# A graph kernel with listed neighbours: one own and four shared gather slots a block in place of three and two

## The chip, the cores and the metric

The kernel runs on one core of one Trainium2 chip. The metric is device time in microseconds of one execution. Three runs of the kernel before gave 667.77, 664.38 and 665.90 us; the median is 665.9 us. The core's engines are named as in the profile: PE (TensorE, matmul), ACT (ScalarE), DVE (VectorE), POOL (GpSimd) and SP (SyncE, which only issues DMAs here).

## The reference

A graph of 4096 nodes with 512 features and an adjacency matrix of 4096 x 4096 integers, in which an entry is 1 with probability 0.000976562, so that a row has four neighbours on average. Two layers, each followed by a residual and a layer normalization:

```python
# layer 0: graph attention, 8 heads of 64
Wh = jnp.einsum('nf,hfo->hno', x, W)
f1 = jnp.einsum('hno,ho->hn', Wh, a[:, :F_OUT])
f2 = jnp.einsum('hno,ho->hn', Wh, a[:, F_OUT:])
e = jax.nn.leaky_relu(f1[:, :, None] + f2[:, None, :], ALPHA)
e = jnp.where(adj[None, :, :] > 0, e, NEG_INF)
attn = jax.nn.softmax(e, axis=-1)
out = jnp.einsum('hnm,hmo->hno', attn, Wh)
x = layernorm(x + out)                     # heads side by side
# layer 1: neighbour mean
mask = (adj > 0).astype(x.dtype)
deg = jnp.sum(mask, axis=1, keepdims=True)
agg = mask @ x / jnp.maximum(deg, 1.0)
combined = jnp.concatenate([x @ W_self + b_self, agg @ W_nb + b_nb], axis=-1)
x = layernorm(x + relu(combined @ W_comb + b_comb))
```

## The kernel before

The kernel never multiplies by the adjacency matrix. It turns each row of it into a list of at most 16 neighbours and then fetches the neighbours' rows from a table in DRAM. If a list doesn't fit, a flag is set and a dense version (`dense_layers`) runs after it; with these inputs it doesn't.

**Blocks and slots.** The 4096 nodes are 32 blocks of 128, one node per partition. For each block the kernel issues five gathers (`gather`, L628, through `rows_of`, L618): each is an indirect DMA that POOL issues and that fetches one table row into each of the 128 partitions, into one of five slots of a buffer `g`. The first `K0 = 3` slots are a node's own: neighbour 1, 2 and 3 of the node that sits on the partition. The last `KH = 2` slots are shared: all further neighbours of the block's first 64 nodes are packed one after another into the 128 places of the first shared slot, those of the other 64 into the second. For each shared place the kernel keeps who owns it (`es`), and the matrix `own` with a 1 where place p belongs to node c lets PE add the shared rows to their owners.

**Stage 1, the lists** (L930 to L968, and the rest up to L1006). Per block, SP loads 2 MB of adjacency, ACT turns it into a mask with a row sum (`mask_adj`, L424), PE folds it into keys (`fold_adj`, L438) and DVE takes the largest ones (`max_keys`). For every four blocks `decode` (L461) makes the lists: it counts the degrees, computes where each node's further neighbours start (the matmul with `triuh`), builds a placing matrix of 128 x 256 per block (L517, L518), and moves the entries into their shared places with one matmul per block and shared slot (L524). `own` is stored as bytes (L547). Beside that, PE computes the table rows of layer 0 (`node_half`, L371): eight values f2, then 512 features; they are stored in the DRAM table `t0`.

**Stage 2, attention** (the loop at L1023). It is a software pipeline written out by hand: iteration i works on blocks i - 1 to i + 6, and each engine runs its instructions in the order in which they are written. For a block, in the order of the data:
- five gathers into one of `GA = 5` buffers; `gather(i + 6)` is issued after the shared matmuls of block i + 1, whose buffer it takes;
- DVE: `a_weights` (L648) adds f1 and f2 and applies the leaky ReLU;
- ACT: `a_exp` (L653) takes the exponential twice: of all five slots into the PSUM tile `ew`, and of the shared slots into the buffer's first eight columns;
- DVE: `a_weigh` (L665) multiplies two slots by their weights, in place, called once for the shared and once for own slots 2 and 3; `a_first` (L672) multiplies own slot 1 into the PSUM tile `num`; `a_own_sum` (L684) and `a_adds` (L689) add the own weights and rows;
- PE: `a_shared` (L696) adds the shared rows, for each half of the columns and each shared slot one matmul whose output is 64 partitions (`tile_position=(0, k * HP)`);
- DVE: `a_recip`; ACT: `a_scale` (L711) divides the eight heads, one instruction each; DVE: `a_moments`; ACT: `root` and `norm` (L727 to L739);
- PE and ACT: transposes of the normalized block (`transposed`, L347), the product with the neighbour weights (`a_z`, L741), stored in table `t1`.

In this stage PSUM's eight banks are `num` (two tiles of two banks), one `ew`, one `tp`, two `pw`.

**Stage 3, layer 1** (L1077 on; the loop at L1133). Five gathers from `t1` per block into one of `GB = 7` buffers. ACT copies own slot 1 into PSUM (`g_first`, L755), DVE adds own slots 2 and 3 (`g_adds`, L759) and makes the owners' matrix (`owners`, L607), PE adds the shared rows (`g_shared`, L781) to the bias and to the product with the self weights (`g_self`, L774), DVE combines both (`g_moments`, L799) and ACT normalizes (`g_norm`). A gather of block b + 7 is issued after `g_adds` of block b. For the first six blocks, gathers are issued during stage 2 for the rows of `t1` that exist by then (`gather_early`), and the missing rows are added later (`g_late`).

A gather waits for whoever last read the slot that it fills: in stage 3 that is ACT for the first slot, DVE for the second and third, PE for the shared ones.

Of the kernel before, what the change touches and what calls it, by code (L numbers as in the profile page):

```python
# [31 lines left out]
F32 = mybir.dt.float32  # L32
BF16 = mybir.dt.bfloat16
# [3 lines left out]
OP = mybir.AluOpType  # L37
# [3 lines left out]
P = 128  # L41
# [8 lines left out]
K0 = 3  # L50
KH = 2
# [62 lines left out]
def listed_layers(  # L114
# [58 lines left out]
    triuh = const.tile([P, P], BF16, name="triuh")  # L173
    nc.vector.tensor_copy(triuh, triu)
    nc.vector.memset(triuh[0:HP, HP:P], 0.0)
    slot = const.tile([P, KH], F32, name="slot")
    for k in range(KH):
        for c in range(KH):
            nc.vector.memset(slot[k * HP : (k + 1) * HP, c : c + 1], float((k + c) * P))
    iota = const.tile([P, KH * P + 1], F32, name="iota")  # L180
    nc.gpsimd.iota(
        iota, [[1, KH * P + 1]], base=0, channel_multiplier=0,
        allow_small_or_imprecise_dtypes=True,
    )
    pidx = const.tile([P, KH], F32, name="pidx")
    nc.gpsimd.iota(
        pidx, [[P, KH]], base=0, channel_multiplier=1, allow_small_or_imprecise_dtypes=True
# [62 lines left out]
    es = const.tile([P, NB, KH, EX], F32, name="es")  # L250
# [210 lines left out]
    def decode(b0, dp, place):  # L461
# [46 lines left out]
        nc.tensor.matmul(po, lhsT=triuh, rhs=nx, start=True, stop=True)  # L508
        nc.vector.tensor_scalar(L[:, :, KL], po, slot[:, 0:1], None, OP.add)
# [3 lines left out]
        for b in range(b0, b0 + G):  # L513
            io, off, en = iota[:, 0 : KH * P], lst[:, b, KL : KL + 1], end[:, b : b + 1]
            lt = dp.tile([P, KH * P], F32, name="lt", bufs=1)
            st = place(b)
            nc.vector.tensor_scalar(lt, io, en, None, OP.is_lt)  # L517
            nc.vector.scalar_tensor_tensor(st, io, off, lt, OP.is_ge, OP.mult)  # L518
            sts.append(st)
            yield  # L520
        pe = ps.tile([P, G, KH, EX + H], F32, name="sm", bufs=2)
        for g in range(G):
            for k in range(KH):
                nc.tensor.matmul(  # L524
                    pe[:, g, k, :], lhsT=sts[g][:, ts(k, P)], rhs=lst[:, b0 + g, K0:],
                    start=True, stop=True,
                )
        nc.vector.tensor_copy(es[:, bs], pe[:, :, :, 0:EX])
        nc.vector.tensor_copy(f1s[:, bs, K0:KS, :], pe[:, :, :, EX:])
        kx = dp.tile([P, G, KH], F32, name="kx", bufs=1)  # L530
        nc.vector.tensor_tensor(
            kx, pidx.unsqueeze(1).to_broadcast([P, G, KH]), es[:, bs, :, KX], OP.subtract
        )
# [6 lines left out]
        nc.vector.tensor_mul(  # L540
            jk, jk, es[:, bs].rearrange("p g k c -> p (g k) c")[:, :, 0:KX]
        )
# [9 lines left out]
            es[:, bs, :, KX + 2 : KX + 3].to_broadcast([P, G, KH, HP]),  # L552
# [4 lines left out]
    def late_lists(dp, place):  # L557
# [21 lines left out]
        for b in range(NE):  # L579
            lt = dp.tile([P, KH * P], F32, name="lt", bufs=1)  # L580
            nc.vector.tensor_scalar(lt[:, 0:P], iota[:, 0:P], endl[:, b : b + 1], None, OP.is_lt)
            nc.vector.scalar_tensor_tensor(
                place[:, b, :], iota[:, 0:P], tl[:, b, KL : KL + 1], lt[:, 0:P], OP.is_ge, OP.mult
            )
            if b % 2:
                yield
# [20 lines left out]
    def owners(b, pool):  # L607

        s = pool.tile([P, KH, P], F32, name="own", bufs=4)[:, :, 0:HP]
        for k in range(KH):  # L610
            E = es[:, b, k, :]
            nc.vector.tensor_scalar(
                s[:, k, :], iota[:, 1 + k * HP : 1 + (k + 1) * HP], E[:, KX + 2 : KX + 3],
                E[:, KX + 1 : KX + 2], OP.is_equal, OP.mult,
            )
        return s
# [27 lines left out]
    def a_owners(b, wp):  # L644
        OWN[b] = wp.tile([P, KH, P], F32, name="own", bufs=4)[:, :, 0:HP]
        nc.scalar.copy(OWN[b], own[:, b])  # L646
# [6 lines left out]
    def a_exp(b):  # L653

        e = E[b]
        w = E[b] = ps.tile([P, KS, H], F32, name="ew")
        nc.scalar.activation(w, e, AF.Exp)
        nc.scalar.activation(G0[b][:, K0:KS, 0:H], e[:, K0:KS, :], AF.Exp)
# [25 lines left out]
    def a_own_sum(b):  # L684
        nc.vector.tensor_reduce(
            NM[b][:, 0:H], E[b][:, 0:K0, :].rearrange("p k h -> p h k"), AX.X, OP.add
        )

    def a_adds(b):  # L689
        for k in range(1, K0):  # L690
            nc.vector.tensor_add(  # L691
                halves_of(NM[b]), halves_of(NM[b]),
                G0[b][:, k, H:TW].rearrange("p (a c) -> p a c", a=2),
            )
# [16 lines left out]
    def a_scale(b):  # L711

        for h in range(H):
            a, q = divmod(h, H // 2)
            o = a * HD + (1 - a) * H + q * D
            s = NM[b][:, o : o + D]
            nc.scalar.mul(s, s, RD[b][:, h : h + 1])  # L717

# [36 lines left out]
    def g_first(b, g):  # L755
        Y[b] = ps.tile([P, HD], F32, name="sm", bufs=2)
        nc.scalar.copy(Y[b], g[:, 0, 0:HD])

    def g_adds(b, g, wp):  # L759
        yp = Y[b]  # L760
        nc.vector.tensor_add(yp, yp, g[:, 1, 0:HD])
        Y[b] = wp.tile([P, HD], F32, name="y", bufs=2)
        nc.vector.tensor_add(Y[b], yp, g[:, 2, 0:HD])  # L763
# [17 lines left out]
    def g_shared(b, g):  # L781
        for a in range(2):
            for k in range(KH):
                r = slice(a * HH, (a + 1) * HH)
                nc.tensor.matmul(
                    NM[b][ts(k, HP), r], lhsT=OWN[b][:, k, :], rhs=g[:, K0 + k, r],
                    start=False, stop=True, tile_position=(0, k * HP), skip_group_check=True,
                )
# [10 lines left out]
    def g_moments(b):  # L799
        yp = ps.tile([P, HD], F32, name="sm", bufs=2)  # L800
        nc.vector.scalar_tensor_tensor(  # L801
            yp, Y[b], lst[:, b, KL + 1 : KL + 2], NM[b], OP.mult, OP.add
        )
        mu = MV[b] = small.tile([P, 1], F32, name="ln_sum")
        nc.vector.scalar_tensor_tensor(
            Y[b], yp, 0.0, xs[:, b, :], OP.max, OP.add, accum_out=mu
        )
# [111 lines left out]
    def on_own(b):  # L919
        return wp.tile([P, KH * P], F32, name="own", bufs=4)  # L920
# [4 lines left out]
    last = oo.tile([P, G, KH * P], F32, name="last")  # L925
# [81 lines left out]
    ps.stage(dict(num=2, ew=1, tp=1, pw=2), dict(sm="tp", mp="pw"))  # L1007
# [15 lines left out]
    for i in range(-3, NB + 2):  # L1023
# [13 lines left out]
        if on(i + 2):  # L1037
            a_first(i + 2)
            a_weigh(i + 2, slice(1, K0))
            a_own_sum(i + 2)  # L1040
            a_adds(i + 2)
# [7 lines left out]
        if i == 21:  # L1049
            lists = [late_lists(dp, last.rearrange("p g (a k) -> p (g a) k", a=2))]  # L1050
# [46 lines left out]
    for b in range(2):  # L1097
        g_bias(b)
        g_first(b, G1[b])
        g_shared(b, G1[b])  # L1100
        g_adds(b, G1[b], wq)
# [22 lines left out]
    nc.vector.tensor_scalar(bad[:, 2, :], end, slot[:, 1:2], None, OP.is_gt)  # L1124
# [8 lines left out]
    for b in range(NB):  # L1133
        if b > 1:
            g_first(b, G1[b])
# [11 lines left out]
        if b > 1:  # L1147
            g_adds(b, G1[b], wq)
            if b + GB < NB:
                G1[b + GB] = gather(t1, b + GB, gps[b % GB])  # L1150
            if b + 2 < NB:
                OWN[b + 2] = owners(b + 2, wp)
        g_moments(b)
# [403 lines left out]
```

## Time and profile before

| What | us |
|---|---|
| median of three runs | 665.9 |
| profiled execution, its own time | 773.3 |
| its span, first to last instruction | 771.6 |
| stage 1, to about | 215 |
| start of attention | 215 to 284 |
| attention | 284 to 500 |
| layer 1, start | 500 to 571 |
| layer 1, with gathers | 571 to 733 |
| layer 1, last blocks | 733 to 771 |

The profiled execution is 107 us longer than the median. In the lines of the profile a line number is that of the kernel before; `out<-in` are the program's names; `x` counts instructions; after the bar stand the busy time in all, the mean of one in nanoseconds, and the idle time of the engine just before these instructions with what ended most of it. In a listing in order of time the first number is the start, the second the duration, and the bracket at the end holds the idle time before it and its releaser. "issue" is a wait that nothing in the profile explains, "remote" one whose release was not recorded. Issuing a DMA is not counted as busy time, except for POOL's indirect ones, where the busy time is that of generating the descriptors and not of the transfer.

### The profile page before, as it was taken

What the parts mean: (1) busy time and instruction counts of PE and PEld (TensorE: products, weight loads), DVE (VectorE), ACT (ScalarE), POOL (GpSimd) and SP (SyncE); (2) the same over time, 40 slices, a digit from 0 to 9 for tenths busy, and PEclk for the clock granted to TensorE, in tenths of its full rate; (3) what the DMA queues carried; (4) which work ended last, traced back from release to release, by engine and by line L of the source; (5) the groups of instructions that cost most, each with busy time, mean ns of one, the idle gap of its engine ahead of it and who ended that gap; (6) DMA issues with size and microseconds to landing.
All of it is one profiled execution on the core that took longest, in us unless ns stands there. A gap on an engine that the chain in (4) does not pass through costs nothing.

```text
span 771.6 us, 9266 instructions
## 1 busy us (share of the span) xinstructions
PE 592.0 (77%) x2358; PEld 312.3 (40%) x2358; DVE 461.5 (60%) x1267; ACT 490.6 (64%) x1313; POOL 354.4 (46%) x474
## 2 busy tenths in 40 slices
PE   5799889889975277877779867956599678877783
PEld 2466666656632033333334333423243223333231
DVE  6256868677743589876788879503036433444373
ACT  3688888889650377887778879722045444554484
POOL 4111121111247565655666752574526666766600
PEclk9899999999998579988889989888799889888997
DMA  8999999999987478897777874685548777888741
GB/s 274 404 408 408 407 408 408 409 408 400 406 291 209 135 222 257 235 319 247 236 235 227 263 228 162 222 268 180 171 123 273 238 255 256 277 262 260 252 161 59
DMA packets 92038, 209.65 MB, mean 272 GB/s; under 512 B 13694, under 2 KB 13702, under 8 KB 91978
## 3 DMA queue, kind: packets, MB, share of 16 engines
q0 software_dynamic: 28624, 94.39, 40.0%
q1 hardware_dynamic: 63024, 114.05, 39.7%
q10 hardware_dynamic: 330, 0.54, 0.2%
q8 instruction: 21, 0.34, 0.2%
q14 instruction: 39, 0.32, 0.1%
HBM read 175.25 MB, written 33.69 MB: 271 GB/s over the span
## 4 chain that ended last, share of the span: by engine, by line
ACT 23%; PE 21%; DMA 18%; another core or an unknown queue 17%; DVE 10%; issue 9%; SPq 1%; ACTq 0%; DVEq 0%
DMA at<-in_adj_dram 16%; ACT num L717 6%; PE tp L312 4%; ACT ab L426 3%; PE pw L744 3%; PE pw L374 3%; PE pw L776 3%; ACT xs L739 3%; ACT xs L730 2%; PE nm L776 2%; DVE sm L801 2%; ACT xT L359 2%; DVE y L763 2%; ACT ln_rs L733 1%
## 5 line engine op out<-in xcount | busy, mean ns | idle before, releaser
L619 POOL DMA_INDIRECT g<-t,idx x290 | 277.6, 957 | 173.1 <-issue 78.1
L744 PE MATMUL pw<-wr,xT 128*128 128x512 f32 x256 | 141.8, 705 | 42.7 <-ACT xT L359 31.7
L426 ACT ACTIVATE ab<-at 128x2048 bf16<-128x2048 int32 x64 | 122.5, 1915 | 34.2 <-DMA at<-in_adj_dram 32.0
L374 PE MATMUL pw<-w_sb,xT 128*128 128x264 f32 x512 | 130.4, 400 | 6.4 <-issue 3.8
L374 PEld LDWEIGHTS pw<-w_sb,xT 128*128 128x128 f32 x512 | 94.6, 194 | 33.3 <-issue 7.1
L744 PEld LDWEIGHTS pw<-wr,xT 128*128 128x128 f32 x256 | 54.8, 225 | 116.1 <-issue 77.9
L381 POOL COPY lst<-row 128x8 f32<-128x8 f32 x32 | 6.6, 205 | 164.8 <-DVE row L378 164.8
L776 PE MATMUL nm<-m,xT 128*128 128x512 f32 x128 | 66.1, 664 | 18.7 <-DMA xT<-xt 13.6
L717 ACT ACTIVATE num<-num,rd 128x64 f32<-128x64 f32 x256 | 73.1, 286 | 9.5 <-DVE rd L709 2.1
L667 DVE TENSOR_TENSOR g<-g,ew 128x1024 f32<-128x1024 f32 x64 | 77.5, 1212 | 0.2
L776 PE MATMUL pw<-m,xT 128*128 128x512 f32 x128 | 64.6, 651 | 16.5 <-DMA xT<-xt 15.2
L801 DVE SCALAR_TENSOR_TENSOR sm<-y,lst,nm 128x512 f32<-128x512 f32 x16 | 12.1, 753 | 84.8 <-remote 37.7
L701 PE MATMUL num<-g,own 128*64 128x264 f32 (+1 forms) x256 | 37.8, 419 | 27.8 <-ACT own L646 15.8
L378 DVE COPY row<-pw 128x264 f32<-128x264 f32 x64 | 27.3, 427 | 34.4 <-PE pw L374 24.2
L776 PEld LDWEIGHTS nm<-m,xT 128*128 128x128 f32 x128 | 26.1, 213 | 52.9 <-issue 31.7
L691 DVE TENSOR_TENSOR num<-num,g 128x512 f32<-128x512 f32 x64 | 44.8, 699 | 2.2
L776 PEld LDWEIGHTS pw<-m,xT 128*128 128x128 f32 x128 | 25.5, 208 | 50.1 <-issue 32.9
L353 PE MATMUL tp<-ident,xs 128*128 128x128 f32 x256 | 40.6, 283 | 6.6 <-ACT xT L366 2.4
L748 ACT COPY row<-pw 128x512 f32<-128x512 f32 x32 | 18.7, 586 | 41.5 <-remote 25.4
L353 PEld LDWEIGHTS tp<-ident,xs 128*128 128x128 f32 x256 | 31.9, 146 | 30.6 <-issue 16.6
L619 POOL DMA_INDIRECT g<-t,idxe x30 | 28.5, 949 | 27.1 <-DVE rd L709 12.3
L767 ACT COPY nm<-brow 128x512 f32<-128x512 f32 x16 | 9.4, 585 | 45.8 <-issue 23.3
(221 smaller groups left out, 951.2 us busy)
## 6 DMA issues: line engine op xcount, KB each, us to landing
at<-in_adj_dram SPq DMA_DIRECT2D x64, 1024.0 KB
xt<-xT SPq DMA_DIRECT2D x32, 256.0 KB
t<-row SPq DMA_DIRECT2D x32, 256.0 KB
xT<-xt SPq DMA_DIRECT2D x32, 256.0 KB
out_dram<-row SPq DMA_DIRECT2D x32, 256.0 KB
t<-row POOLq DMA_DIRECT2D x31, 260.0 KB
xs<-in_x_dram SPq DMA_DIRECT2D x31, 256.0 KB
g<-t,idx POOLq DMA_INDIRECT x290
```

Of the source, the lines that this page charges most:

```text
L312: nc.tensor.matmul(mp, lhsT=wT[:, d, :], rhs=wc[:, d, :], start=(d == 0), stop=(d == FB - 1))
L353: nc.tensor.transpose(tp[:, c, :], xs[:, b, ts(c, P)], ident)
L374: nc.tensor.matmul(pw, lhsT=xT[:, c, :], rhs=w_sb[:, c, k * HW : (k + 1) * HW], start=(c == 0), stop=(c == FB - 1),)
L426: nc.scalar.activation(ab, loads.pop((b, h)), AF.Relu, accum_out=asum[:, b, h : h + 1])
L619: nc.gpsimd.indirect_dma_start(out=out, out_offset=None, in_=table, in_offset=bass.IndirectOffsetOnAxis(ap=at, axis=0),)
L667: nc.vector.tensor_tensor(gv, gv, E[b][:, sl].unsqueeze(3).to_broadcast([P, sl.stop - sl.start, H, D]), OP.mult,)
L691: nc.vector.tensor_add(halves_of(NM[b]), halves_of(NM[b]), G0[b][:, k, H:TW].rearrange("p (a c) -> p a c", a=2),)
L701: nc.tensor.matmul(NM[b][ts(k, HP), a * HD : a * HD + r.stop - r.start], lhsT=OWN[b][:, k, :], rhs=G0[b][:, K0 + k, r], start=False, stop= ...
L717: nc.scalar.mul(s, s, RD[b][:, h : h + 1])
L744: nc.tensor.matmul(pz, lhsT=xT[:, c, :], rhs=m2[:, c, :], start=(c == 0), stop=(c == FB - 1))
L776: nc.tensor.matmul(NM[b], lhsT=xT[:, c, :], rhs=m1[:, c, :], start=False, stop=(c == FB - 1), skip_group_check=True,)
L801: nc.vector.scalar_tensor_tensor(yp, Y[b], lst[:, b, KL + 1 : KL + 2], NM[b], OP.mult, OP.add)
```

## The change

`K0` becomes 1 and `KH` 4: a node has one own slot, and each quarter of a block (32 nodes) has one shared slot of 128 places. The number of gathers stays five. `KX`, the length of the shared part of a list, grows from 13 to 15.

- `decode`: the placing matrix is 128 x 128 for all four slots together. To keep the slots apart, the lists are first multiplied by `part`, which is 1 for a row's own quarter, into `lq`; one matmul per block then fills all four slots.
- `a_exp`: one exponential, from `e` into the first eight columns of the gathered buffer, which is in SBUF; `ew` is gone, and its PSUM bank becomes a second `tp`. `a_weigh` is called once, for the four shared slots; it and `a_first` read the weights from the buffer.
- `a_adds` and `g_adds` are gone; `a_own_sum` is a copy.
- `a_shared` and `g_shared`: matmuls with an output of 32 partitions at four column positions, eight in attention, four of 512 columns in layer 1 (before: four of 264 or 256).
- `a_scale`: ACT divides four heads, DVE the other four in one instruction.
- Layer 1: `g_moments` reads own slot 1 straight from the gathered buffer, except for blocks 0 and 1, where `g_first` copies it into SBUF; so the gather of block b + 7 is now issued after `g_moments` of block b. `owners` is two instructions over all four slots.

```diff
-K0 = 3
-KH = 2
+K0 = 1
+KH = 4
...
-        po = ps.tile([P, G], F32, name="sm", bufs=2)
-        nc.tensor.matmul(po, lhsT=triuh, rhs=nx, start=True, stop=True)
-        nc.vector.tensor_scalar(L[:, :, KL], po, slot[:, 0:1], None, OP.add)
+        nc.tensor.matmul(po, lhsT=triuq, rhs=nx, start=True, stop=True)
+        nc.vector.tensor_copy(L[:, :, KL], po)
...
-            io, off, en = iota[:, 0 : KH * P], lst[:, b, KL : KL + 1], end[:, b : b + 1]
-            lt = dp.tile([P, KH * P], F32, name="lt", bufs=1)
+            io, off, en = iota[:, 0:P], lst[:, b, KL : KL + 1], end[:, b : b + 1]
+            lt = dp.tile([P, P], F32, name="lt", bufs=1)
...
+        lq = dp.tile([P, G, KH, EX + H], F32, name="lq", bufs=1)
+        nc.vector.tensor_tensor(
+            lq, lst[:, bs, K0:].unsqueeze(2).to_broadcast([P, G, KH, EX + H]),
+            part.unsqueeze(1).unsqueeze(3).to_broadcast([P, G, KH, EX + H]), OP.mult,
+        )
         pe = ps.tile([P, G, KH, EX + H], F32, name="sm", bufs=2)
         for g in range(G):
-            for k in range(KH):
-                nc.tensor.matmul(
-                    pe[:, g, k, :], lhsT=sts[g][:, ts(k, P)], rhs=lst[:, b0 + g, K0:],
-                    start=True, stop=True,
-                )
+            nc.tensor.matmul(
+                pe[:, g].rearrange("p k c -> p (k c)"), lhsT=sts[g],
+                rhs=lq[:, g].rearrange("p k c -> p (k c)"), start=True, stop=True,
+            )
...
     def owners(b, pool):
-        s = pool.tile([P, KH, P], F32, name="own", bufs=4)[:, :, 0:HP]
-        for k in range(KH):
-            E = es[:, b, k, :]
-            nc.vector.tensor_scalar(
-                s[:, k, :], iota[:, 1 + k * HP : 1 + (k + 1) * HP], E[:, KX + 2 : KX + 3],
-                E[:, KX + 1 : KX + 2], OP.is_equal, OP.mult,
-            )
+        s = pool.tile([P, KH, HP], F32, name="own", bufs=4)
+        nc.vector.tensor_tensor(
+            s, iota[:, 1 : P + 1].rearrange("p (k c) -> p k c", k=KH),
+            es[:, b, :, 1:2].to_broadcast([P, KH, HP]), OP.is_equal,
+        )
+        nc.vector.tensor_tensor(s, s, es[:, b, :, 0:1].to_broadcast([P, KH, HP]), OP.mult)
...
     def a_exp(b):
-        e = E[b]
-        w = E[b] = ps.tile([P, KS, H], F32, name="ew")
-        nc.scalar.activation(w, e, AF.Exp)
-        nc.scalar.activation(G0[b][:, K0:KS, 0:H], e[:, K0:KS, :], AF.Exp)
+        e, E[b] = E[b], G0[b][:, :, 0:H]
+        nc.scalar.activation(E[b], e, AF.Exp)
...
     def a_scale(b):
-        for h in range(H):
-            a, q = divmod(h, H // 2)
-            o = a * HD + (1 - a) * H + q * D
-            s = NM[b][:, o : o + D]
+        for h in range(H // 2):
+            s = NM[b][:, H + h * D : H + (h + 1) * D]
             nc.scalar.mul(s, s, RD[b][:, h : h + 1])
+        s = NM[b][:, HD : HD + HH].rearrange("p (h d) -> p h d", d=D)
+        nc.vector.tensor_tensor(
+            s, s, RD[b][:, H // 2 :].unsqueeze(2).to_broadcast([P, H // 2, D]), OP.mult
+        )
...
     def g_shared(b, g):
-        for a in range(2):
-            for k in range(KH):
-                r = slice(a * HH, (a + 1) * HH)
-                nc.tensor.matmul(
-                    NM[b][ts(k, HP), r], lhsT=OWN[b][:, k, :], rhs=g[:, K0 + k, r],
-                    start=False, stop=True, tile_position=(0, k * HP), skip_group_check=True,
-                )
+        for k in range(KH):
+            nc.tensor.matmul(
+                NM[b][ts(k, HP), :], lhsT=OWN[b][:, k, :], rhs=g[:, K0 + k, 0:HD],
+                start=False, stop=True, tile_position=(0, k * HP), skip_group_check=True,
+            )
...
-    ps.stage(dict(num=2, ew=1, tp=1, pw=2), dict(sm="tp", mp="pw"))
+    ps.stage(dict(num=2, tp=2, pw=2), dict(sm="tp", mp="pw"))
...
             a_first(i + 2)
-            a_weigh(i + 2, slice(1, K0))
             a_own_sum(i + 2)
-            a_adds(i + 2)
...
         if b > 1:
-            g_first(b, G1[b])
+            Y[b] = G1[b][:, 0, 0:HD]
             g_shared(b, G1[b])
...
         if b > 1:
-            g_adds(b, G1[b], wq)
-            if b + GB < NB:
-                G1[b + GB] = gather(t1, b + GB, gps[b % GB])
             if b + 2 < NB:
                 OWN[b + 2] = owners(b + 2, wp)
-        g_moments(b)
+        g_moments(b, wq)
+        if b > 1 and b + GB < NB:
+            G1[b + GB] = gather(t1, b + GB, gps[b % GB])
```

## The prediction

> **What bounds the kernel now.** I read the page's busy row and its chain first, then busy time by stretch, then the costliest groups, then single instructions in order of time.
>
> ```profile
> PE 592.0 (77%) x2358; PEld 312.3 (40%) x2358; DVE 461.5 (60%) x1267; ACT 490.6 (64%) x1313; POOL 354.4 (46%) x474
> ...
> ACT 23%; PE 21%; DMA 18%; another core or an unknown queue 17%; DVE 10%; issue 9%; SPq 1%; ACTq 0%; DVEq 0%
> ```
>
> No engine is full and the chain changes hands all the time: the stages have different limits. The 17% (some 131 of 771.6 us) are waits whose end no record shows. The profiled execution took 773.3 us and the median is 665.9 us, 107 us less; most of those waits probably belong to the profiling. So I count differences per block in stretches without such a wait, and carry them over one to one.
>
> ```profile
> 284.00:500.00 216.00, 171.72 (x598) 79.97 (x599) 174.10 (x384) 173.07 (x566) 125.03 (x131) 0.88 0.76 238
> 500.00:571.00 71.00, 47.49 (x120) 21.68 (x120) 10.80 (x34) 18.31 (x44) 35.88 (x38) 0.83 0.60 183
> 571.00:733.00 162.00, 128.42 (x394) 52.48 (x392) 73.85 (x164) 81.66 (x208) 107.94 (x114) 0.88 0.81 258
> 733.00:771.00 38.00, 24.31 (x90) 10.19 (x88) 22.53 (x48) 25.21 (x66) 1.21 (x2) 0.89 0.33 111
> ```
>
> Columns: length, then busy PE, PE load, DVE, ACT, POOL, then clock, DMA share, GB/s. The first stretch is layer 0's attention, the last two are layer 1. In attention three engines stand at 0.8. The 215 us ahead of it are adjacency loads at some 400 GB/s; the change adds no byte there.
>
> ```profile
> L619 POOL DMA_INDIRECT g<-t,idx x290 | 277.6, 957 | 173.1 <-issue 78.1 <-remote 19.8 <-ACT sm L757 17.9
> ...
> L717 ACT ACTIVATE num<-num,rd 128x64 f32<-128x64 f32 x256 | 73.1, 286 | 9.5 <-DVE rd L709 2.1
> L667 DVE TENSOR_TENSOR g<-g,ew 128x1024 f32<-128x1024 f32 x64 | 77.5, 1212 | 0.2
> ...
> L691 DVE TENSOR_TENSOR num<-num,g 128x512 f32<-128x512 f32 x64 | 44.8, 699 | 2.2
> ```
>
> An attention block without a stall takes 6.38 us from one normalization to the next (L739 at 340.10 and 346.48, at 418.61 and 424.99). ACT fills it without a gap; DVE has about 6.0 us of work (1.21 + 1.21 + 0.67 + 1.43 + 0.69 and small ones). POOL is as near: a gather is busy 0.95 us and the next starts 0.30 us later ("issue"), so five gathers take 6.25 us. POOL's busy share hides this, since the 0.30 isn't busy. Two engines bound attention within 2% of each other. Layer 1 has the same five gathers a block; where none is left (733 to 771) a block takes 4.7 us, PE's own 3.7 + 1.1.
>
> The lines that decide the case are in the order of time:
>
> ```profile
> 392.07 1.21 DVE L667 TENSOR_TENSOR g<-g,ew 128x1024 f32<-128x1024 f32 x1
> 392.21 0.96 POOL L619 DMA_INDIRECT g<-t,idx  x1 [0.30 <-issue]
> ...
> 422.49 0.74 DVE L331 SCALAR_TENSOR_TENSOR brow<-wc,bcol,brow 128x512 f32<-128x512 f32 x1
> 422.69 1.37 POOL L619 DMA_INDIRECT g<-t,idx  x1 [0.30 <-DVE y L722]
> ...
> 428.02 0.68 DVE L547 TENSOR_TENSOR own<-iota,es 128x512 uint8<-128x512 f32 x1
> 428.12 1.39 POOL L619 DMA_INDIRECT g<-t,idx  x1 [0.30 <-issue]
> ```
>
> A gather that starts inside L667 (one input in SBUF, `ew` in PSUM) takes its usual 0.96 us. One that starts inside L331 or L547, whose two inputs both lie in SBUF, takes 1.37 or 1.39: it ends 0.83 and 0.81 us after the DVE instruction's end, as if it began only then. Six gathers of the trace are so held (also at 230.53, 266.34, 397.22 and 416.10), each to the DVE instruction's end plus 0.81 to 0.83. Gathers that began before the DVE instruction were not delayed (289.51: 0.95), nor was one that began 0.09 us after it (303.54).
>
> **What the Trainium skill says.** SBUF — State Buffer, "Who interferes with whom": DVE and GpSimd share a pair of SBUF ports as an exclusive lock, and "A DVE instruction with two SBUF inputs contends with a GpSimd instruction that reads SBUF"; with at most one SBUF input it doesn't. The page also infers that a tensor_tensor leaves descriptor generation alone; this trace shows the indirect gathers held, so the trace decides. VectorE: DVE Perf Modes, "The perf-mode tier table": fp32 tensor_tensor runs at one element a cycle wherever its operands lie; the trace agrees (1.21 us for 1,024). TensorE: Matmul & The Clock Gate, Part 3: column tiles run concurrently (2.38x measured with three 32-wide ones); the trace has two at once, eight 256-column passes on 64-wide tiles in 1.08 us where a 512-column pass on the full array takes 0.46.
>
> **The change part by part.** Attention, per block:
> - *ACT.* Four of eight divisions go (4 x 0.31 = 1.25 us) and one of two exponentials (0.12 from one start to the next): 6.38 - 1.37 = 5.0 us.
> - *DVE.* Two adds (1.43) go, and a reduce of 0.18 becomes a copy (0.15, estimate). Two multiplications of 1.21 become one of 2,048 elements; 512 more elements cost 1.212 - 0.699 = 0.51, so 1.21 + 2 x 0.51 = 2.24 us. Added: 256 elements of division, about 0.43 (L378 moves 264 out of PSUM in 0.427). 6.0 - 1.43 - 0.03 - 0.18 + 0.43 = 4.8 us. The division waits for ACT's four, and behind it stand the moments and the next block's weights; the loop moments, root and norm (2.64), four divisions (1.25), DVE's division (0.43), moments (0.75), with hand-overs, is 5.4 us.
> - *PE.* Shared rows: eight matmuls on 32-wide tiles instead of four on 64-wide. With four at once, 1.1 us as now; were they to go two at once, 2.0; one at a time, 3.5 (16 passes of 0.22). I take 1.2. With 3.7 for L744 and 0.75 for transposes that is 5.6. The second `tp` bank only loosens this.
> - *POOL.* Still five gathers, 6.25 us; the bytes are the same. But `a_weigh` and `a_first` now read rows and weights both from SBUF: 2.24 + 0.67 us of each block. A gather starts every 1.25 us, so one starts inside each multiplication, on average 0.62 after its start, waits for its end, and then takes 0.83, not 0.95: 2.24 - 0.62 - 0.12 = 1.5 us. `a_first` follows 0.2 later, mostly while the released gather runs: nothing, at most 0.3. The gathers queue behind the held one, five blocks of buffers ahead, so one hold delays no one; a hold in every block cuts the rate.
>
> So POOL's block becomes 6.25 + 1.5 = 7.75 where the phases are free. If the five fall best (starts at 2.24, 3.37, 4.62, 5.87, 7.12, and the next multiplication after that), 7.15. Against 6.38 this is +0.77 to +1.37, times 32 multiplications +25 to +44 us; I take the middle, +34. Below nothing is possible if the gathers aren't held: then POOL's 6.25 bounds, -0.13 x 32 = -4 us.
>
> Layer 1, per block: ACT loses a 0.58 copy, DVE two adds of 0.70; `g_moments` reads one SBUF tensor beside PSUM, so it holds nothing. PE keeps eight passes of twice the columns on four tiles instead of two: 1.1 us if four go at once. Neither ACT (3.9 us) nor DVE (3.3) bounds here, so the 2 us saved are covered by POOL's 6.25 and, at the end, PE's 4.7. `owners` becomes two 128-element instructions with SBUF inputs (0.3 each, by L581): a gather starts in them about every second block and waits 0.15 on average, +2 us in all. The gather moves behind `g_moments`: its first slot waits for DVE's first pass over block b, 0.75 us after PE, but its rows are wanted seven blocks later; nothing, and at worst that 0.75 once while the queue fills.
>
> Stage 1: placing lists halves (L517 and L518 from 256 to 128 elements: 0.36 + 0.48 to 0.30 + 0.35, four a group, -0.8), eight list matmuls become four, the masked copy `lq` adds 0.6. Hidden under the adjacency loads; 3 us are gained between 215 and 284, where lists stand on the chain. Another 4 us for the last attention blocks, which wait for no gather and gain ACT's 1.37.
>
> Sum: +34 + 2 - 3 - 4 = +29: 802 in the profiled execution, 665.9 + 29 = **695 us** for the median. All five slots fit: drawing the adjacency as the reference does puts at most 127 entries into a quarter of a block (98 on average), so the dense path isn't taken.
>
> **The rivals.**
> - *Faster, 643 us.* Outside the profiler a gather may come faster than every 1.25 us. Then the held one is caught up: five gathers plus 1.5 us fit into 6.38 once they come every 0.98 us, and the price is nothing. Below 0.84 PE's 5.6 bounds instead: (6.38 - 5.6) x 32 = 25 us less, with the 2 us of the last blocks and of the lists about 643. For it: the unexplained waits show that profiling costs much. Against: the gap of 0.30 us is the same all over, and 326 gathers of 1.25 us (408 us) fit into the 665.9 - 215 that remain for both layers.
> - *No change, 662 to 668 us.* Gathers come every 1.0 us, or they aren't held and POOL's 6.25 bounds: 0 to -4.
> - *PE's tiles go one at a time, about 740 us.* Attention's PE block is 3.5 + 3.7 + 0.75 = 7.95, layer 1's 3.4 + 3.7 = 7.1: +50 and +25. Against: 64-wide tiles overlap in this trace.
>
> **How the numbers follow.** Held gathers bound attention: 0.60, from 678 to 715. Faster: 0.25, from 635 to 660. No change: 0.10. PE tiles serial: 0.05. The range 646 to 720 leaves out about half of the faster case and the last. A change of 0.5%, 3.3 us, is about what the spread of 664.4 to 667.8 lets one tell. Faster 0.27, same 0.09, slower 0.64.
>
> **What would show it.** In the changed kernel's trace: the mean of the attention gathers rises from 0.957 us to about 1.25, with some 30 of 2 us or more, each ending 0.8 us after a 2.2 us multiplication; ACT's share in attention falls below 0.7 and its idle time lies ahead of waits for DVE; an unstalled block takes 7.1 to 7.8 us. Wrong if gathers keep 0.95 us, if blocks fall below 6.38 us, or if the shared matmuls take over 2 us.

## The result, and the profile after

The changed kernel takes 707.4 us (median of four runs, 704.7 to 708.6) against 665.3 us before (664.4 to 667.8): 1.062 times the time before, with an interval of 1.058 to 1.066. That is 42 us more, where 29 were forecast.

The profile of before that the prediction read came from an execution of 773 us with long waits; below it is called disturbed. So the kernel before was profiled again (run `e0_before`, 667.6 us, span 665.8), and comparisons below use that trace. Three experiments ran on a chip on which every run of the kernel before takes 780 to 799 us and whose traces show long waits too; it is called the disturbed chip, and they are read against before on that same chip. All ratios are of the faster runs of both kernels, so that on the disturbed chip, where the runs spread, they differ from the quotient of the two medians.

The busy row of the page, first of before (undisturbed), then of after:

```profile
PE 560.0 (84%) x2358; PEld 299.6 (45%) x2358; DVE 460.2 (69%) x1267; ACT 491.0 (74%) x1313; POOL 353.4 (53%) x474
```

```profile
PE 574.7 (82%) x2549; PEld 286.1 (41%) x2550; DVE 393.0 (56%) x1150; ACT 440.4 (63%) x1123; POOL 401.1 (57%) x474
```

DVE lost 67 us of work and ACT 51, as meant. POOL has as many instructions as before and 48 us more of busy time. These are gathers; here is their group, of before and of after, in the stretch of the 160 gathers of attention (busy time, mean of one in ns, idle time ahead):

```profile
L619 POOL DMA_INDIRECT g<-t,idx x160 | 153.4, 959 | 55.9 <-issue 21.6 <-ACT wr L316 5.7 <-DMA g<-t,idx 5.2
```

```profile
L619 POOL DMA_INDIRECT g<-t,idx x160 | 196.4, 1228 | 55.6 <-issue 26.2 <-DMA g<-t,idx 8.2 <-DMA t<-row 7.5
```

A gather of attention takes 1.228 us in the mean instead of 0.959; 30 of them take over 1.6 us. One block in order of time, DVE's instructions and then POOL's (start, duration):

```profile
353.21 2.28 DVE L665 TENSOR_TENSOR g<-g 128x2048 f32<-128x2048 f32 x1
355.41 0.20 DVE L698 RECIPROCAL rd<-num 128x8 f32<-128x8 f32 x1
355.53 0.67 DVE L673 TENSOR_TENSOR num<-g 128x512 f32<-128x512 f32 x1
```

```profile
352.15 0.95 POOL L619 DMA_INDIRECT g<-t,idx  x1 [0.30 <-PE num L690]
353.42 2.90 POOL L619 DMA_INDIRECT g<-t,idx  x1 [0.30 <-issue]
356.62 0.95 POOL L619 DMA_INDIRECT g<-t,idx  x1 [0.30 <-DMA g<-t,idx]
```

The multiplication runs from 353.21 to 355.49; the gather that starts 0.21 us into it ends at 356.32, 0.83 us after its end. All 30 gathers of attention that start inside this multiplication are held like that: each ends 0.82 or 0.83 us after the multiplication's end, whether it started 0.08 or 1.23 us into it. DVE then waits for what is late. Its first instruction of a block, in attention, before and after:

```profile
L650 DVE TENSOR_TENSOR e<-g,f1s 128x40 f32<-128x40 f32 x29 | 5.7, 195 | 5.0 <-DMA g<-t,idx 3.4 <-issue 1.4
```

```profile
L650 DVE TENSOR_TENSOR e<-g,f1s 128x40 f32<-128x40 f32 x31 | 6.2, 199 | 45.8 <-DMA g<-t,idx 33.9 <-issue 11.7
```

The idle time ahead of it grows from 5 to 46 us: gathers set attention's pace now.

In after's trace POOL never rests from its first gather to its last: of 325 gaps between gathers, 324 are the 0.30 us of "issue", one is 1.9. So the time divides at the first gather, the last one of attention and the last one of all. Busy time by stretch, with these cuts, first before, then after:

```profile
220.50:424.10 203.60, 158.77 (x603) 74.17 (x602) 179.94 (x417) 167.68 (x541) 153.37 (x160) 0.93 0.89 283
424.10:650.40 226.30, 210.49 (x702) 91.19 (x700) 131.90 (x301) 150.35 (x395) 157.50 (x167) 0.98 0.84 282
650.40:665.80 15.40, 2.57 (x8) 1.23 (x8) 3.18 (x7) 5.02 (x14) 0.00 (x0) 0.58 0.24 82
```

```profile
229.50:474.40 244.90, 180.40 (x874) 81.77 (x873) 168.59 (x390) 147.66 (x441) 196.43 (x160) 0.87 0.78 239
474.40:687.80 213.40, 203.00 (x668) 74.47 (x668) 76.61 (x205) 118.11 (x305) 161.21 (x166) 1.00 0.89 293
687.80:702.60 14.80, 3.14 (x8) 0.41 (x6) 1.45 (x3) 4.93 (x14) 0.02 (x1) 0.75 0.25 84
```

| Stretch | before | after | change | forecast |
|---|---|---|---|---|
| until the first gather | 220.5 | 229.5 | +9.0 | -3 |
| gathers of attention | 203.6 | 244.9 | +41.3 | +34 |
| gathers of layer 1 | 226.3 | 213.4 | -12.9 | +2 - 4 |
| after the last gather | 15.4 | 14.8 | -0.6 | |
| span | 665.8 | 702.6 | +36.8 | +29 |

The medians differ by 42; the profiled execution of after was the fastest of its four. Two of the four changes have a sign that was not forecast: the start and layer 1. The experiments take the 41.3 first.

### The profile page after: what moved, and what is told of

The parts are those of the page before. It is cut to its first block, busy times and chain, and to the rows that moved or that the text cites. A ratio compares the mean times of both kernels' runs of the same rounds, so it can differ in the third digit from the quotient of the medians.

```text
span 702.6 us, 9267 instructions
## 1 busy us (share of the span) xinstructions
PE 574.7 (82%) x2549; PEld 286.1 (41%) x2550; DVE 393.0 (56%) x1150; ACT 440.4 (63%) x1123; POOL 401.1 (57%) x474
## 5 line engine op out<-in xcount | busy, mean ns | idle before, releaser
L619 POOL DMA_INDIRECT g<-t,idx x290 | 320.4, 1105 | 96.9 <-issue 48.8
L427 ACT ACTIVATE ab<-at 128x2048 bf16<-128x2048 int32 x64 | 122.5, 1915 | 41.3 <-DMA at<-in_adj_dram 41.0
L735 PE MATMUL pw<-wr,xT 128*128 128x512 f32 x256 | 132.8, 667 | 11.8 <-ACT xT L360 11.8
L704 ACT ACTIVATE num<-num,rd 128x64 f32<-128x64 f32 x128 | 36.8, 287 | 59.2 <-DVE rd L698 56.0
L665 DVE TENSOR_TENSOR g<-g 128x2048 f32<-128x2048 f32 x32 | 73.1, 2285 | 0.0
L690 PE MATMUL num<-g,own 128*32 128x256 f32 (+1 forms) x512 | 38.5, 421 | 41.7 <-issue 30.2
L761 PE MATMUL nm<-m,xT 128*128 128x512 f32 x128 | 58.8, 602 | 0.3 <-DMA xT<-xt 0.3
L690 PEld LDWEIGHTS num<-g,own 128*32 128x32 f32 x512 | 15.5, 115 | 55.1 <-issue 35.7
L784 DVE SCALAR_TENSOR_TENSOR sm<-g,lst,pw 128x512 f32<-128x512 f32 x15 | 11.3, 755 | 46.7 <-PE pw L768 37.3
L784 DVE SCALAR_TENSOR_TENSOR sm<-g,lst,nm 128x512 f32<-128x512 f32 x15 | 11.3, 755 | 46.6 <-PE nm L768 34.9
L721 ACT ACTIVATE row<-y,ln_sum 128x512 f32<-128x512 f32 x32 | 23.1, 721 | 20.2 <-DVE y L789 20.2
## 6 DMA issues: line engine op xcount, KB each, us to landing
at<-in_adj_dram SPq DMA_DIRECT2D x64, 1024.0 KB, 11.3
```

Source lines behind the costliest of these rows:

```text
L427: nc.scalar.activation(ab, loads.pop((b, h)), AF.Relu, accum_out=asum[:, b, h : h + 1])
L619: nc.gpsimd.indirect_dma_start(out=out, out_offset=None, in_=table, in_offset=bass.IndirectOffsetOnAxis(ap=at, axis=0),)
L665: nc.vector.tensor_tensor(gv, gv, E[b][:, sl].unsqueeze(3).to_broadcast([P, sl.stop - sl.start, H, D]), OP.mult,)
L690: nc.tensor.matmul(NM[b][ts(k, HP), a * HD : a * HD + r.stop - r.start], lhsT=OWN[b][:, k, :], rhs=G0[b][:, K0 + k, r], start=False, stop= ...
L721: nc.scalar.activation(wide, Y[b], AF.Square, bias=MV[b], scale=-float(HD), accum_out=rs)
L735: nc.tensor.matmul(pz, lhsT=xT[:, c, :], rhs=m2[:, c, :], start=(c == 0), stop=(c == FB - 1))
```

## Experiments on the held gathers

The theory: a gather that starts inside a DVE instruction with two SBUF inputs waits for its end, and POOL's queue sets the pace of attention. The rivals: the chain of ACT's and DVE's divisions with the moments behind it sets the block; or something else in the new slots does.

**The kernel before, again** (`e0_before`, no edit).

> The kernel before, profiled once more, because its first profile holds some 107 us that its timed runs don't have. Both theories: about 666 us, and a span close to that. Held-gather theory: in attention the gathers stand every 1.25 us with no hold (mean 0.95 to 0.97 us), five of them about 6.3 us, a block about 6.4 us; the first gather starts at about 220 us, as in the disturbed profile.

Measured: as expected, mean 0.959 us; between most groups of five gathers 6.25 to 6.29 us. Waits whose release was not recorded ("remote"), 76 us of DVE's in layer 1 alone in the first profile, are not in this one at all.

**The weights in PSUM again, all else as changed.** PSUM's eighth bank has to come from the second `tp`.

```diff
-        e, E[b] = E[b], G0[b][:, :, 0:H]
-        nc.scalar.activation(E[b], e, AF.Exp)
+        e = E[b]
+        w = E[b] = ps.tile([P, KS, H], F32, name="ew")
+        nc.scalar.activation(w, e, AF.Exp)
+        nc.scalar.activation(G0[b][:, K0:KS, 0:H], e[:, K0:KS, :], AF.Exp)
...
-    ps.stage(dict(num=2, tp=2, pw=2), dict(sm="tp", mp="pw"))
+    ps.stage(dict(num=2, ew=1, tp=1, pw=2), dict(sm="tp", mp="pw"))
```

> The changed kernel with the attention weights put back into PSUM (bank ew, one bank tp instead of two); one own and four shared slots, the wide multiplication and the divided scaling stay. Held-gather theory: L665 then reads one SBUF tensor and no gather is held; the 160 attention gathers fall from 1.23 us to 0.95 to 0.97, 160 x 0.27 = 43 us go, 707 - 43 = 664 us (655 to 672). Rival, the chain of divisions and the DVE work queued behind it sets a block's length: 700 to 710 us.

Measured: 669.7 us, 38 less than the changed kernel; 1.011 of before (1.005 to 1.017). The group of attention's gathers, and one block in order of time:

```profile
L619 POOL DMA_INDIRECT g<-t,idx x160 | 153.5, 960 | 57.4 <-issue 27.4 <-DMA g<-t,idx 11.1 <-ACT ab L427 7.3
```

```profile
350.63 2.28 DVE L667 TENSOR_TENSOR g<-g,ew 128x2048 f32<-128x2048 f32 x1
```

```profile
350.62 0.94 POOL L619 DMA_INDIRECT g<-t,idx  x1 [0.30 <-PE num L692]
351.87 0.95 POOL L619 DMA_INDIRECT g<-t,idx  x1 [0.30 <-issue]
353.13 0.96 POOL L619 DMA_INDIRECT g<-t,idx  x1 [0.30 <-ACT xs L732]
```

The multiplication is the same 2.28 us on the same 2,048 elements, and the gather that starts inside it at 351.87 takes 0.95. Of attention's gathers 52 start inside a multiplication here, and none of them takes over 1.05. Attention's gathers take 203.6 us, as before the change. The Trainium skill, SBUF — State Buffer, "Who interferes with whom", puts the line between one SBUF input and two for instructions outside what it calls the 2-port perf modes, and this pair of runs agrees; its inference about descriptor generation, which the prediction names, doesn't hold for the gathers of after. The total is 6 us above the middle of what was expected: with POOL no longer late, layer 1's gathers take 218.5 us and not the 213.4 of the changed kernel, for a reason that the experiments on the queue show.

**One transpose bank, weights in SBUF**: the control for the bank (`tp=1` is the whole edit).

> Control of the run with the weights in PSUM, which also gave up the second transpose bank: the changed kernel with one bank tp instead of two, weights in SBUF. Held-gather theory: the bank is loose, 704 to 711 us, and gathers of 2 us and more stay. If the bank were what changed the time: 690 us or less, or 715 or more.

Measured, on the disturbed chip: 781.4 us (775.6 to 797.4) against 790.3 (780.0 to 799.5) of before there, a ratio of 0.995 (0.992 to 0.998). The totals expected can't be judged there. What can is the hold: 160 gathers of 1.242 us in the mean, 30 over 1.6 us, as with two banks. So the bank isn't what freed the gathers. The ratio suggests that where other waits leave POOL idle, as they do there (19 us of gaps at once, then 3 to 5 us every 22 us in layer 1), held gathers cost little; no run isolates that.

**The kernel before with its weights in SBUF**: the same exchange of `a_exp` the other way, three own and two shared slots.

> The kernel before with one edit: the attention weights stay in SBUF beside the rows, as in the changed kernel; three own and two shared slots stay. Held-gather theory: two multiplications of 1.21 us and the first one of 0.67 us now hold gathers, about 1.35 us a block less 0.1 us of slack: 32 x 1.25 = 40 us, 705 us (690 to 715), with gathers of 1.2 us and more. Rival, the slots and the divisions are what costs: one exponential goes and nothing is added, 660 to 668 us.

Measured: 677.7 us, 1.020 of before (1.015 to 1.026). The hold comes with the weights' place alone:

```profile
L619 POOL DMA_INDIRECT g<-t,idx x160 | 179.2, 1120 | 54.7 <-issue 21.9 <-DMA g<-t,idx 8.5 <-ACT wr L316 5.8
```

But the total rises by 14 us and not by 40, outside the range expected. The hold is 160 x (1.120 - 0.959) = 26 us, 0.8 a block and not 1.35. Of the 59 gathers of attention that start inside one of these multiplications 48 are held, each again to 0.82 or 0.83 us after its end; but a multiplication of 1.21 us ends sooner than one of 2.28, and only 6 gathers took over 1.6 us. `a_first`, which the expectation counted in full, held one. Attention's gathers take 228.1 us (+24.5). Those of layer 1 take 211.5, 14.8 less than in before: most of the loss comes back there. The experiments on the queue below take that up.

**The wide multiplication in four pieces**, weights in SBUF.

```diff
-            a_weigh(i + 2, slice(K0, KS))
+            for k in range(K0, KS):
+                a_weigh(i + 2, slice(k, k + 1))
```

> The changed kernel with the wide multiplication cut into four of 512 elements, weights still in SBUF; it adds 4 x 0.70 - 2.29 = 0.5 us of VectorE work a block. Held-gather theory, with the gather let in between two instructions: each hold ends with the piece, so 0.6 to 0.7 us a block instead of 1.4: 707 - 24 = 683 us (672 to 692), no gather over 1.6 us. If the hold lasts over all pieces: 710 us or more, gathers still of 2 us and more. Rival, VectorE's chain sets the block: 707 to 725 us.

Measured: 672.9 us, 1.015 of before (1.010 to 1.020), at the lower edge of what was expected. A piece takes 0.69 us (116 of them in attention), no gather takes over 1.47, and the mean is

```profile
L619 POOL DMA_INDIRECT g<-t,idx x160 | 161.4, 1008 | 55.9 <-issue 26.2 <-DMA g<-t,idx 8.8 <-ACT ab L427 7.4
```

so the hold is 0.25 us a block where 0.6 to 0.7 was expected, although the four pieces read two SBUF inputs for longer (2.53 us in the block below) than the one instruction did. The longest hold of this run, DVE's pieces merged into one line, then POOL:

```profile
413.80 2.53 DVE L665 TENSOR_TENSOR g<-g 128x512 f32<-128x512 f32 x4
```

```profile
413.84 1.47 POOL L619 DMA_INDIRECT g<-t,idx  x1 [0.30 <-DVE e L650]
415.61 0.95 POOL L619 DMA_INDIRECT g<-t,idx  x1 [0.30 <-issue]
416.87 0.98 POOL L619 DMA_INDIRECT g<-t,idx  x1 [0.30 <-issue]
```

The gather that starts 0.04 us into the first piece ends at 415.31, 0.82 us after that piece's end (413.80 + 0.69) and while the third runs. Of the 59 gathers that start inside a piece, 21 take over 1.05 us, each ending 0.82 or 0.83 us after its own piece. The others take 0.94 to 1.00: they start within 0.02 us of a piece's start or in its last 0.2 us. So the gather isn't slowed but shut out until the end of the instruction in which it starts, and that end is enough even where the next instruction of the same kind follows at once.

**All eight divisions on ACT**, weights in SBUF.

```diff
-        for h in range(H // 2):
-            s = NM[b][:, H + h * D : H + (h + 1) * D]
+        for h in range(H):
+            a, q = divmod(h, H // 2)
+            o = a * HD + (1 - a) * H + q * D
+            s = NM[b][:, o : o + D]
             nc.scalar.mul(s, s, RD[b][:, h : h + 1])
-        s = NM[b][:, HD : HD + HH].rearrange("p (h d) -> p h d", d=D)
-        nc.vector.tensor_tensor(
-            s, s, RD[b][:, H // 2 :].unsqueeze(2).to_broadcast([P, H // 2, D]), OP.mult
-        )
```

> The changed kernel with all eight divisions on ScalarE again, weights in SBUF. Held-gather theory: GpSimd's queue sets the block at 7.65 us, ScalarE has 6.3 us of work in it, VectorE loses 0.43: no change, 704 to 711 us. Rival, ScalarE's divisions, VectorE's division behind them and the moments behind that set the block: it moves by 32 x 0.4 = 13 us or more either way, below 697 or above 717.

Measured: 705.4 us (703.8 to 709.1), the changed kernel's time. 128 divisions of 0.288 us, 37 us, put back on ACT cost nothing, so neither engine's divisions set the block while the gathers are held. This part of the change is worth nothing here.

## Experiments on the queue and on layer 1

If POOL's queue already bounds attention in the kernel before, a gather more in a block must cost its 1.25 us without any hold.

**A gather repeated in each attention block of before**, into the place of the block's last one.

```diff
+        if table.shape[1] == TW:
+            rows_of(g[:, KS - 1, 0:TW], table, idx[:, b, KS - 1 : KS])
         return g
```

> The kernel before with one gather more in each attention block, a repeat of its last slot into the same place. It prices GpSimd's queue by itself, without any hold. Queue theory: 32 x 1.25 = 40 us more in the queue, of which the waits that the kernel before has at the change of layers and in layer 1 (21 us of gaps above 0.30 us in all, some 8 of them in attention's blocks) take back 10 to 15: first gather 220, attention 243 us, layer 1 213 us, end 15 us later: 692 us (686 to 698). If the queue had slack in attention: 664 to 672 us.

Measured, on the disturbed chip: 866.9 us, 1.107 of before there (1.100 to 1.114). The experiment failed by its edit: the repeat fills the place of the gather just ahead of it, so it waits for that one's landing, and POOL stands still for 2.9 to 3.6 us ahead of nearly every repeat. It prices that wait and not the queue.

**The same with buffers of its own**, which nobody reads, in 29 blocks:

```diff
             G0[i + 1 + GA] = gather(t0, i + 1 + GA, gps[(i + 1 + GA) % GA])
+            rows_of(wq.tile([P, TW], F32, name="xg", bufs=2), t0, idx[:, i + 1 + GA, 0:1])
```

> The kernel before with one gather more in 29 of the attention blocks, into two buffers of its own that nobody reads, so that it waits for no landing of the gather just before it. Queue theory: 29 x 1.25 = 36 us more in GpSimd's queue; attention from the first to the last of its gathers 203.6 - 3 + 36 = 237 us; at the change of layers the 12 us gap and some smaller ones shrink and give 10 to 14 us back, so the total rises by 20 to 26 us over the kernel before of the same chip, 684 to 690 us where that takes 664. If the queue had slack in attention's blocks: within 5 us of the kernel before.

Measured: 688.5 us, 1.036 of before (1.032 to 1.041), 24 us more than the 664.7 of before in the same runs. The two groups in attention:

```profile
L619 POOL DMA_INDIRECT g<-t,idx x160 | 153.3, 958 | 56.4 <-issue 25.3 <-ACT wr L316 5.8 <-DMA g<-t,idx 5.2
L619 POOL DMA_INDIRECT xg<-t,idx x29 | 27.8, 958 | 8.8 <-issue 5.5 <-DMA g<-t,idx 3.0 <-PE pw L744 0.3
```

Attention's gathers take 240.5 us (219.8 to 460.3), 36.9 more than before's, which is 1.27 us for each of the 29. The added transfers aren't what costs: the DMA engines are busy for 0.87 of the stretch, against 0.89 in before, and POOL goes from gather to gather with only two waits above its 0.30 us (0.7 and 2.0). So POOL's queue has next to no slack in before's attention; with a gather every 0.98 us, as one rival had it, the 29 would have fitted in. And again layer 1 gives back: its gathers take 209.6 us, 16.7 less.

Where it comes from shows at the change of layers. POOL in order of time, before:

```profile
423.18 0.95 POOL L619 DMA_INDIRECT g<-t,idx  x1 [0.30 <-issue]
436.03 0.94 POOL L619 DMA_INDIRECT g<-t,idxe  x1 [11.91 <-DVE rd L709]
...
443.83 0.94 POOL L619 DMA_INDIRECT g<-t,idxe  x1 [1.83 <-DVE num L685]
...
454.07 0.94 POOL L619 DMA_INDIRECT g<-t,idxe  x1 [4.29 <-DVE num L691]
```

and after:

```profile
473.43 0.95 POOL L619 DMA_INDIRECT g<-t,idx  x1 [0.30 <-issue]
474.68 0.95 POOL L619 DMA_INDIRECT g<-t,idxe  x1 [0.30 <-ACT row L739]
475.94 0.95 POOL L619 DMA_INDIRECT g<-t,idxe  x1 [0.30 <-PE tp L590]
```

Before, the other engines are as slow as POOL within 2% (a block takes 203.6 / 32 = 6.36 us, five gathers 6.25), and at the end of attention POOL is some buffers ahead: it waits 11.9, 1.8 and 4.3 us for buffers that they still use. The last product of attention ends 46.5 us after its last gather (470.6 against 424.1). After, they wait for POOL; the last product ends 28.4 us after the last gather (502.8 against 474.4), the buffers are free, and the early gathers of layer 1 follow at once. Beyond the usual 0.30 us between gathers, POOL waits 18.2 us after attention's last gather in before and 1.6 in after, 16.6 less; the gathers there are themselves busy for 3.7 us longer (161.2 against 157.5), and what is left is the 12.9. In the two experiments these waits are 2.2 and 1.5 us. A queue that becomes slower than its readers wins back the waits that it had at the seam: 12.9 us here, 14.8 and 16.7 in the two experiments.

## Experiments on the later start

In the kernels above, the first gather starts some 9 us later wherever there are four shared slots (229.5, 229.7 and 228.9 us in after, with the weights in PSUM and with four pieces) than where there are two (219.8 to 220.5). The page's DMA issues show the same transfers taking longer, before first, then after (KB each, median us to landing):

```profile
at<-in_adj_dram SPq DMA_DIRECT2D x64, 1024.0 KB, 10.7
```

```profile
at<-in_adj_dram SPq DMA_DIRECT2D x64, 1024.0 KB, 11.3
```

From 110 to 205 us the DMA engines move 389 GB/s after, 405 before, and their busy share is the same (1.04 and 1.05). The bytes and the instructions are the same. What differs is where the buffers lie: the compiled program of before has the four adjacency buffers (`at`) at 145,664 and every 8,192 bytes on, multiples of 256; the one of after has them at 143,904 and on, 32 bytes past such a multiple, because the temporaries of `decode` that are laid out beside them grew. The Trainium skill, DMA: Bandwidth & Descriptors, "How a descriptor splits into AXI transactions", says that a transfer's descriptor that doesn't start at a multiple of 256 bytes also fetches the bytes from the boundary below it, and that these unused bytes cost beats (units of 32 bytes). So the address was moved, by an unused tile of 32 bytes per partition, in both kernels:

```diff
     bp = bp_cm.__enter__()
+    bp.tile([P, 8], F32, name="pad8")
```

> The changed kernel with an unused tile of 32 bytes that moves the four adjacency buffers from addresses 32 bytes past a multiple of 256 back to multiples of 256, where the kernel before has them; nothing else moves. Alignment theory of the 9 us that the first gather starts later in the changed kernel (229.5 against 220.5 us, loads at 392 against 408 GB/s): first gather at 220 to 222 us, total 707 - 9 = 698 us (694 to 702). Rival, the list work with the masked copy and fewer matmuls is what is late: first gather at 229, total 704 to 710 us.

Measured: 702.1 us (700.3 to 703.8), 5 less than the changed kernel. Loads land in 10.7 us again, and the first gather starts at 222.7.

> The kernel before with the same unused tile of 32 bytes, which moves its adjacency buffers off the multiples of 256; no instruction changes. Alignment theory: first gather at about 229 us, total 664 + 9 = 673 us (668 to 676). Rival, addresses don't matter: 220 us and 662 to 667 us.

Measured: 673.5 us, 1.014 of before (1.012 to 1.017), 9 more than before. Not one instruction is changed; the first gather starts at 227.1, and the loads:

```profile
at<-in_adj_dram SPq DMA_DIRECT2D x64, 1024.0 KB, 11.3
```

Of all buffers in SBUF the tile moves only these four. The two runs show in both directions that the address delays the start, by 6.8 us in the changed kernel and by 6.6 in before. It is not all of the 9.0: with the buffers at multiples of 256 the kernels with four shared slots still start at 221.9 to 223.0, some 2 us later than those with two. The list work is the rival named for that, and no run isolates it. By what mechanism a start off a multiple of 256 costs 4% of the rate they don't show. In the changed kernel the whole gain is 5 us and not 9: the start wins 6.8, but the same holds fell a little worse (mean of attention's gathers 1.253 instead of 1.228, 4 us in all).

**Both causes taken away**: weights in PSUM, and the tile.

> The changed kernel with the attention weights in PSUM and the 32-byte tile together. Both causes taken away: 669.7 - 9 = 661 us (656 to 665), at or below the kernel before. If the two overlap, that is, if the later start is absorbed somewhere, 665 to 670 us.

Measured: 661.3 us (median of ten), 0.996 of before, with an interval of 0.994 to 0.998. The two costs add up: 669.7 less 8.4. This is the fastest version of the slots, and it beats the kernel before by only 3 us, though DVE and ACT have much less to do in it (392 and 443 us of work against 460 and 491): POOL's 1.25 us a gather remains.

**The multiplication in pieces, and the tile.**

> The changed kernel with the wide multiplication in four pieces and the 32-byte tile, weights in SBUF: 672.9 - 8 = 665 us (661 to 668), the same as the kernel before. If the two gains overlap, 668 to 673 us.

Measured, on the disturbed chip: 791.6 us, 1.011 of before there (1.006 to 1.016). Attention's gathers have a mean of 1.000 us and the first starts at 223.0, so both remedies work; whether the total meets before's on a chip without those waits is open.

## Why the prediction was right, and where not

Slower was right, and 707 lies between the 695 taken and the upper end of 720. By its steps:

- *The hold: right in mechanism, and nearest to its upper end.* It was read from six gathers of the trace before, and the changed kernel's blocks confirm it, down to the 0.83 us after the multiplication's end. The mean of attention's gathers was to rise to about 1.25 us (it is 1.228), some 30 of 2 us or more were to appear (27, and two more among layer 1's), a block was to take 7.15 to 7.75 (244.9 / 32 = 7.65). The term of +34 measured +41.3: the middle between the best and the free phase was taken, and the phases fell nearly as if free. A held gather starts 0.74 us into the multiplication in the mean (0.62 was assumed for free phases), and the hold is 43 us in all, 1.35 a block. Two readings of the first trace were too narrow. A gather that began 0.09 us after the DVE instruction was taken as not delayed (303.54), but in after those at 274.80 and 453.96 begin 0.08 us after the multiplication and take 3.03 us. And a seventh gather was held there: the one at 279.29 takes 1.10 us and ends 0.82 after L476, a DVE instruction with one input, in SBUF.
- *Layer 1 and the last blocks, +2 and -4: this step failed in size.* The differences were counted block by block, each against the bound of its own stage. Layer 1's own edits did cost little: 3.0 of the 3.7 us of longer gathers there are two that attention's last multiplications hold, which leaves 0.7 for the holds that were put at 2. But the seam between the stages was left out, although the first trace has its waits of POOL too: 12.3, 1.9 and 4.6 us after the last gather of attention. With POOL late they nearly vanish, and 12.9 us of the 41 come back.
- *The lists, -3 (forecast between 215 and 284 us): this step failed in sign.* It priced the instructions of stage 1 and held that the stage, bound by loads, gets no byte more. True, and the start still came 9.0 us later: 6.8 of them because the same bytes landed off a multiple of 256, and some 2 that no run isolates. Neither the diff nor the order of instructions shows the 6.8; the addresses in the compiled program do.
- *PE.* Eight matmuls on four column tiles were taken at 1.2 us; they take 1.09, and layer 1's four of twice the columns 1.07. One tile at a time would have been 3.5 by the prediction's own sum, so the four go together, and the serial rival falls. The wide multiplication was put at 2.24 us (2.285), DVE's division at 0.43 (0.432).
- *The faster rival* (gathers come faster outside the profile) falls by the 29 extra gathers. It rested on the 107 us by which the first profile exceeded the median, and on the step that most of those waits probably belong to the profiling. That step was wrong: an undisturbed profile of before takes 667.6 us; the waits belong to the chip or the moment. Nothing else was named for this rival, so its chance of 0.25 rested on that step alone. Its 643 doesn't follow from its terms either: 665.9 less 25 and 2 is 639.
- *Carrying the differences over one to one* held for the median, but it isn't safe in general: on the disturbed chip, whose traces have waits like those of the profile that was read, the changed kernel with one transpose bank takes 0.995 of before's time.

In part the closeness of the total is luck: the start and the seam, of which neither was foreseen, nearly cancel. The sum came out 13 us low in the median: 7 from the hold and 12 from the start, less 11 at layer 1 and the end (-13.5 where -2 was forecast), make 8 in the profiled executions, and the rest is the distance of the two profiled executions from their medians.

## What to carry to other kernels

Before moving an operand from PSUM into SBUF, look at what GpSimd does meanwhile: one long VectorE instruction with two SBUF inputs shuts its gathers out until it ends, and if GpSimd's queue is the pace, that can cost more than the work saved, as here; one input in PSUM avoids it, and the same work in short instructions avoids most of it. A queue's busy share hides its pace, so take the distance from start to start (1.25 us at 0.95 busy), and at a seam between stages ask which of two sides waits, for a loss on the one is partly taken out of the other's wait. After a change of buffer sizes, compare the addresses of the buffers of a stage that is bound by loads.

## What the hardware showed that was not expected

- 1 MB loads into buffers that start 32 bytes past a multiple of 256 land in 11.3 us, into buffers at a multiple in 10.7 (389 against 402 to 405 GB/s between 110 and 205 us); at 224 bytes past, in the kernel before with the tile, the same 11.3 (391 GB/s).
- The hold ends at the end of each VectorE instruction even where the next, of the same kind, follows with no idle time: in four pieces of 0.69 us it falls from 1.35 to 0.25 us a block.
- Two SBUF inputs are not the only case. L476 of before (L477 of after) is a TENSOR_SCALAR on 384 integers with one input, in SBUF, and its output in SBUF too. In all traces together five gathers start well inside it, and all five end 0.82 us after it, having taken 1.09 or 1.10 us.
